# One root for layer 1's feed forward, and layer 2's twofold normalization moved into that feed forward

## The chip, the core and the metric

The kernel runs on one core of a Trainium2 chip. Its time is the device time of one execution in microseconds (us). The engines work side by side, each through its own list of instructions in order: TensorE (PE; its weight loads are shown as PEld), VectorE (DVE), ScalarE (ACT), GpSimd (POOL), and SyncE (SP), which issues the DMAs here. Semaphores tie the lists together.

## The reference

Four layers, each an attention-like part and a feed forward, every part added to `x` (4 batches, 1024 tokens, 128 features) after a layer normalization of `x`. What matters here is the end of layer 1 and the start of layer 2:

```
x = x + silu((LN(x) @ W_Q) @ W1 + b1) @ W2 + b2        # layer 1's outputs, with the trained W1, b1, W2, b2
g = softmax(LN(x) @ gate_w + gate_b)                    # 8 experts
g = where(g >= 0.1, g, 0); g = g / sum(g)
x = x + sum_e g[e] * (LN(x) @ expert_w[e] + expert_b[e]) # layer 1's feed forward
x = x + attention(LN(LN(x)) * gamma + beta)             # layer 2: normalized twice
```

W1, b1, W2 and b2 come out of a training loop over the sequence that runs just before (layer 1's "rounds").

## The kernel before

`x` stays on chip as 32 tiles of 128 tokens by 128 features; eight tiles are a batch. Beside it lies `xnT`, the normalized tokens turned so that features lie on partitions, which the matmuls read. All matrices are float32.

**A normalization** of one batch has two halves. `ln_moments` gets the sums (`ln_sums`: eight statistics instructions, L134, and five small operations, L137 to L141, on DVE), then the root: one ACT instruction (L114) and a reciprocal on DVE (L115), and `nm`, the shift (L125). With `twice` (layer 2) the second normalization is folded into the factor: six small operations on DVE (L117 to L122), a root on ACT (L123), and `nm`. `ln_scale` then scales eight tiles, four on ACT (L154) and four on POOL (L152), turns them on PE (L158, eight transposes into two PSUM tiles), and ACT copies the two results into `xnT` (L164, or L162 with gamma and beta). `self.ahead` keeps the sums that were made early.

**Layer 1's outputs** are the last part of `l1_attn`, in pools of their own (`l1o`, `l1q`). A preamble multiplies W_Q by W1 (L686 to L692) and spreads b2 (L694 to L700). Then eight blocks of 512 tokens: a product `hp` (L703), Silu on ACT (L705), b2 added on POOL (L169), four products `op` (L709), and the addition to `x` on DVE (`add_four`, L173).

**Layer 1's feed forward**, `l1_ffn`, opens its pools after that: two PSUM banks for transposes, one each for gates (`gp`), turned gates (`ap`) and biases (`bp`), three for experts (`ep`). For each batch it computes the gates (`weights`: sixteen-pass product L1014, then a softmax and threshold of small DVE operations L1019 to L1059, with Exp on ACT, L1024), adds the weighted biases (`biases`: L1065, L1067, L1070, L173), and for each of the eight tiles multiplies by all eight experts in two halves (L1081). Of the eight results, five are accumulated into `x` by DVE (L1090), three are weighted by ACT into `sc` (L1088) and added by POOL (L1092). The normalization of batch b + 1 stands ahead of batch b's tiles in the program.

**Layer 2's attention** begins with `layernorm(twice=...)`, again with its own pools (`ln`, `ln_ps`), and then projects batch 0 (L1205).

The order on each engine inside these parts is made by a planner: it takes the program's order as priority, and issues an instruction earlier where, by its own costs, an engine is free and the inputs and buffers are there. A pool opened later reuses the memory of a closed one, so its first writes wait for the last readers there. The attention itself is in an order written out by hand. ACT holds one table of functions at a time: Silu, Sqrt and Exp each have one; Copy and Identity run under any. A change of table is an instruction of its own (ACT_TABLE_LOAD), put before the function that needs it.

## Time and profile before

| | |
|---|---|
| median of 3 runs | 2631.39 us (2629.13 to 2631.81) |
| profiled execution | 2639.67 us |
| its span, first to last instruction | 2638.0 us |
| mean granted PE clock | 0.927 |
| first and last `op` product of layer 1's outputs (L709) | 827.8 and 841.4 us |
| first scaling of layer 1's feed forward (L154) | 846.84 us |
| first and last expert product (L1081) | 853.6 and 944.9 us |
| layer 2's first projection (L1205) | 957.24 us |

A group's row in the profile names line, engine, operation, output and inputs, how often, and the mean time of one. A row of a timeline begins with start and duration in us; several instructions of one kind in a row are merged (x8), and the brackets at the end say how long the engine had been idle before and what ended that. Lines are those of the kernel before; L158 and the like are helpers that several layers call.

ACT loads a table nine times between 818 and 924 us: at 818.24 (copy), 823.88 (Silu), 844.62 (root), 852.86 (Exp), 857.12 (root), 858.74 (Exp), 867.31 (root), 892.12 (Exp) and 923.23 (root), 1.28 us each.

### The profile page before, as it was taken

How to read it: one execution, taken by the hardware profiler on the slowest of the kernel's cores; microseconds unless marked ns; L12 is line 12 of the kernel's file. 1: busy time of each engine (PE TensorE's matmuls, PEld its weight loads, DVE VectorE, ACT ScalarE, POOL GpSimd, SP SyncE). 2: the span in 40 equal slices, each digit the busy share in tenths (PEclk: the TensorE clock that was granted, in tenths of full speed). 3: DMA queues.
4: the chain of work that ended last, by engine and by line, in shares of the span. 5: the costliest groups of instructions: out<-in, count | busy, mean ns of one | idle time of the engine just before them, and what ended most of it. 6: DMA issues, size and time to landing. Idle time of an engine off the chain costs nothing.

```text
span 2638.0 us, 51055 instructions
## 1 busy us (share of the span) xinstructions
PE 2384.1 (90%) x19913; PEld 1216.0 (46%) x19913; DVE 1793.4 (68%) x3670; ACT 1497.1 (57%) x3333; POOL 291.6 (11%) x525
## 2 busy tenths in 40 slices
PE   5688768899997979999999779999999999999878
PEld 4455435599996434333333443333333333333256
DVE  5889878466675767767775358767777777777343
ACT  4466458555554443666666635666666666656722
POOL 6012021000002440000000340000000000000011
PEclk8699879899998889999999879999999999999968
DMA  1333230000000000100010000000000000000000
GB/s 45 74 76 75 68 82 1 1 1 2 1 1 2 1 8 10 22 14 14 14 19 6 5 5 10 8 10 9 8 9 11 10 8 8 11 8 8 5 17 18
DMA packets 116719, 46.66 MB, mean 18 GB/s; under 512 B 88473, under 2 KB 111097, under 8 KB 116474
## 3 DMA queue, kind: packets, MB, share of 16 engines
q1 hardware_dynamic: 116474, 43.35, 8.3%
q8 instruction: 159, 2.61, 0.4%
q14 instruction: 86, 0.70, 0.1%
HBM read 17.04 MB, written 12.98 MB: 11 GB/s over the span
## 4 chain that ended last, share of the span: by engine, by line
PE 55%; DVE 4%; ACT 2%; POOL 1%; issue 1%; SPq 0%; DMA 0%; POOLq 0%; DVEq 0%; ACTq 0%
PE pb L1320 30%; PE po L1357 16%; PE pa L1265 2%; DVE bm L1277 1%; ACT es L1325 1%; PE pp L1205 1%; PE pe L1320 1%; DVE bm L1304 1%; PE pv L1186 1%; PE tp L158 1%; PE rp L1762 1%; PE gp L1014 1%; DVE bm L1308 0%; PE pr L1617 0%; PE kp L1530 0%
## 5 line engine op out<-in xcount | busy, mean ns | idle before, releaser
L1325 ACT ACTIVATE es<-pb 128x512 f32<-128x512 f32 x1462 | 795.7, 595 | 496.1 <-PE pb L1320 339.3
L1320 PE MATMUL pb<-q,k 32*128 32x512 f32 x2924 | 905.8, 640 | 3.2 <-DVE bm L1308 1.7
L1265 PE MATMUL pa<-k,q 32*128 32x512 f32 x2944 | 844.4, 648 | 10.2 <-DMA q<-q 10.2
L1277 DVE TENSOR_REDUCE bm<-pa 128x2 f32<-128x1024 f32 x496 | 604.6, 1224 | 260.5 <-PE pb L1320 168.0
L1357 PE MATMUL po<-es,v 128*32 128x256 f32 (+1 forms) x5760 | 474.8, 405 | 0.0
L1320 PEld LDWEIGHTS pb<-q,k 32*128 32x128 f32 x2924 | 295.3, 183 | 325.7 <-ACT es L1325 170.4
L1357 PEld LDWEIGHTS po<-es,v 128*32 128x32 f32 x5760 | 117.2, 108 | 528.7 <-issue 489.3
L1273 DVE TENSOR_REDUCE bm<-pa 128x16 f32<-128x1024 f32 x240 | 293.0, 1221 | 97.3 <-PE pb L1320 60.7
L1265 PEld LDWEIGHTS pa<-k,q 32*128 32x128 f32 x2944 | 233.5, 186 | 36.8 <-issue 18.5
L152 POOL TENSOR_SCALAR xn<-x,rs,nm 128x128 f32<-128x128 f32 x112 | 49.6, 459 | 1187.9 <-DVE nm L125 1013.7
L366 DVE TENSOR_TENSOR pr<-T,L 128x31 f32<-128x31 f32 (+15 forms) x248 | 91.7, 370 | 27.9 <-DMA L<-ld 20.6
L369 DVE TENSOR_TENSOR T<-T,pr 128x31 f32<-128x31 f32 (+15 forms) x248 | 93.1, 376 | 8.5
L158 PE MATMUL tp<-ident,xn 128*128 128x128 f32 x224 | 46.3, 357 | 42.5 <-ACT xn L154 38.0
L1364 DVE COPY oT<-po 128x512 f32<-128x512 f32 x48 | 32.7, 682 | 64.7 <-PE po L1357 64.7
L821 ACT ACTIVATE w<-tr,half 128x128 f32<-128x128 f32 x128 | 47.1, 368 | 48.3 <-PE tr L819 45.6
L796 ACT ACTIVATE a<-hp,wb 128x128 f32<-128x128 f32 x128 | 47.1, 368 | 41.6 <-PE hp L792 40.1
L1081 PE MATMUL ep<-L_ffn_expert_w,xnT 128*128 128x512 f32 x128 | 66.7, 653 | 3.3 <-DVE x L1090 3.0
L324 PE MATMUL wide<-bt,kt 32*128 32x128 f32 x512 | 30.4, 365 | 43.0 <-DVE mt L413 30.9
L486 PE MATMUL sp<-ux,kn 128*128 128x256 f32 x128 | 46.2, 494 | 17.8 <-ACT ux L475 17.7
L158 PEld LDWEIGHTS tp<-ident,xn 128*128 128x128 f32 x224 | 33.8, 178 | 60.4 <-ACT xn L154 46.9
L804 DVE TENSOR_TENSOR dlt<-gr,mask 128x128 f32<-128x128 f32 x96 | 28.0, 291 | 48.4 <-PE gr L802 48.1
L853 ACT COPY dr<-tr 128x128 f32<-128x128 f32 x128 | 34.1, 266 | 43.2 <-PE tr L851 41.1
(469 smaller groups left out, 3695.4 us busy)
## 6 DMA issues: line engine op xcount, KB each, us to landing
ld<-kk SPq DMA_DIRECT2D x128, 32.0 KB
L<-ld SPq DMA_DIRECT2D x8, 512.0 KB
td<-T SPq DMA_DIRECT2D x8, 512.0 KB
tb<-td SPq DMA_DIRECT2D x128, 32.0 KB
md<-nt SPq DMA_DIRECT2D x192, 2.0 KB
q<-md SPq DMA_DIRECT2D x192, 2.0 KB
x<-in_L_attn_x_dram SPq DMA_DIRECT2D x4, 512.0 KB
od<-o SPq DMA_DIRECT2D x32, 64.0 KB
```

The lines of the kernel that those rows point to most:

```text
L152: nc.gpsimd.tensor_scalar(xn[:, i, :], src[:, i, :], sl, bl, ALU.mult, ALU.add)
L158: nc.tensor.transpose(tp[:, i, :], xn[:, 4 * n + i, :], self.ident)
L366: nc.vector.tensor_mul(pv, T[:, 0 : j + 1, j : j + 1].to_broadcast(sh), L[:, j : j + 1, j + 1 :].to_broadcast(sh))
L369: nc.vector.tensor_sub(T[:, 0 : j + 1, j + 1 :], T[:, 0 : j + 1, j + 1 :], pv)
L796: nc.scalar.activation(self.a, self.hp, AF.Silu, bias=B1)
L1081: nc.tensor.matmul(ep.rearrange("p a b -> p (a b)"), lhsT=self.tok(t), rhs=ew[:, 4 * h : 4 * h + 4, :].rearrange("p a b -> p (a b)"), star ...
L1265: nc.tensor.matmul(pa[:, j % 2, :], lhsT=st["q"][r, i * P : (i + 1) * P], rhs=st["k"][r, n * 512 : (n + 1) * 512], start=True, stop=True,)
L1273: nc.vector.tensor_reduce(out[:, :, 1:9], pa.rearrange("p j (c s) -> p j c s", c=8), axis=AX.X, op=ALU.max)
L1277: nc.vector.tensor_reduce(out[:, :, n : n + 1], pa, axis=AX.X, op=ALU.max)
L1320: nc.tensor.matmul(pb, lhsT=st["k"][r, kc * P : (kc + 1) * P], rhs=st["q"][r, n * 512 : (n + 1) * 512], start=True, stop=True,)
L1325: nc.scalar.activation(es[turn][:, j, :], pb, AF.Exp, scale=scale)
L1357: nc.tensor.matmul(po[r, cols], lhsT=vring[b % 2][:, kc, 4 * g + j, :], rhs=es[:, j, cols], start=kc == 0, stop=True, skip_group_check=True,)
```

## The change

Layer 1's outputs move from `l1_attn` into a function `l1_out`, which gets the pools of the feed forward: `hp` uses the three `ep` buffers, `op` alternates between the buffers of `ap` and `bp`, and the preamble uses `gp`, `ap` and `bp`, with all its copies on DVE. `l1_ffn` calls it for two blocks (one batch) at a time, and after each batch takes that batch's sums. A new `ln_roots` makes the factors of several batches at once: one root, one reciprocal, one `nm` over all their columns. The feed forward's four normalizations use it with all four batches.

Layer 2's twofold normalization leaves `l2_attn`. The sums of batches 0 and 1 are taken in the feed forward during batches 1 and 2. After batch 2's tiles, `ln_roots` runs for batches 0 to 2 (with the sums of batch 2), and these three are scaled and turned ahead of batch 3's biases and tiles in the program. Batch 3 follows after its own tiles. These use the feed forward's pools: two PSUM banks for transposes in place of four.

```diff
+    def ln_roots(self, pool, bs, twice=None):
+        nc = self.nc
+        for b in bs:
+            if b not in self.ahead:
+                self.ln_sums(pool, b)
+        for b in bs:
+            del self.ahead[b]
+        rs, nm = (pool.tile([P, len(bs), TPB], F32, tag=f"{t}{len(bs)}", name=t) for t in ("rs", "nm"))
+        own = slice(bs[0], bs[-1] + 1)
+        q = self.sums[:, 1, own, :]
+        if twice is None:
+            nc.scalar.activation(rs, q, AF.Sqrt, bias=self.eps, scale=1.0 / D)
+            nc.vector.reciprocal(rs, rs)
+        else:
+            nc.vector.tensor_scalar(rs, q, 1.0 / D, EPS, ALU.mult, ALU.add)
+            nc.vector.reciprocal(rs, rs)
+            nc.vector.tensor_mul(q, q, rs)
+            nc.vector.tensor_scalar(q, q, 1.0 / D, EPS, ALU.mult, ALU.add)
+            nc.vector.reciprocal(q, q)
+            nc.vector.tensor_mul(rs, rs, q)
+            nc.scalar.activation(rs, rs, AF.Sqrt)
+        nc.vector.scalar_tensor_tensor(nm, self.sums[:, 0, own, :], -0.5, rs, ALU.mult, ALU.mult)
+        return [(rs[:, i, :], nm[:, i, :]) for i in range(len(bs))]
...
-        with tc.tile_pool(name="l1o", bufs=2) as two, tc.tile_pool(name="l1q", bufs=2, space=PSUM) as ps:
...
+    def l1_out(self, one, two, ps):
...
+        wqT = turned("gp", wq, [P, D])
+        b2r = turned("bp", B2, [1, D])
+        wp = ps.tile([P, D], F32, tag="ap", name="wp", bufs=1)
+        nc.tensor.matmul(wp, lhsT=wqT, rhs=W1, start=True, stop=True)
...
+        bp = ps.tile([P, D], F32, tag="gp", name="bp", bufs=1)
...
+        def batch(b):
+            for n in (2 * b, 2 * b + 1):
+                hp = ps.tile([P, 512], F32, tag="ep", name="hp", bufs=3)
                 nc.tensor.matmul(hp, lhsT=qw, rhs=self.tok(4 * n, 512), start=True, stop=True)
-                a = two.tile([P, 512], F32, tag="a", name="a")
+                a = two.tile([P, 512], F32, tag="a", name="a", bufs=2)
                 nc.scalar.activation(a, hp, AF.Silu, bias=B1)
                 self.add_bias(4 * n, b2)
-                op = ps.tile([P, 4, D], F32, tag="op", name="op")
+                op = ps.tile([P, 4, D], F32, tag=("ap", "bp")[n % 2], name="op", bufs=1)
                 for i in range(4):
                     nc.tensor.matmul(op[:, i, :], lhsT=a[:, i * P : (i + 1) * P], rhs=W2, start=True, stop=True)
                 self.add_four(4 * n, op)
...
-            self.ln_batch(ln, lps, 0)
+            out = self.l1_out(one, two, ps)
+            for b in range(NB):
+                out(b)
+                self.ln_sums(ln, b)
+            by = self.ln_roots(one, range(NB))
+            self.ln_scale(ln, lps, 0, by[0])
             g = weights(0)
             for b in range(NB):
                 if b + 1 < NB:
-                    self.ln_batch(ln, lps, b + 1)
+                    self.ln_scale(ln, lps, b + 1, by[b + 1])
                 biases(b, g)
+                if 0 < b < NB - 1:
+                    self.ln_sums(ln, b - 1)
                 for i in range(TPB):
                     tile_of(b * TPB + i, g[:, i, :])
                     if i == TPB // 2 and b + 1 < NB:
                         ahead = weights(b + 1)
                 g = ahead
+                if b >= NB - 2:
+                    done = range(NB - 1) if b == NB - 2 else (b,)
+                    twice = self.a2["gamma"], self.a2["beta"]
+                    by = self.ln_roots(one, done, twice)
+                    for i in done:
+                        self.ln_scale(ln, lps, i, by[i - done[0]], twice)
...
     def l2_attn(self):
         nc, a = self.nc, self.a2
         H, HD = 8, 16
-        self.layernorm(twice=(a["gamma"], a["beta"]))
```

## The prediction

> **What bounds the kernel now.** I read the page first, for the shares and for the clock row; then the table of stretches around the change; then the timelines of single engines there. The chain of waits is of no help for this place: followed back from the end it stops at 981.73 us, in layer 2's attention, so everything before that has to be read from timelines.
>
> ```profile
> PE 2384.1 (90%) x19913; PEld 1216.0 (46%) x19913; DVE 1793.4 (68%) x3670; ACT 1497.1 (57%) x3333; POOL 291.6 (11%) x525
> PEclk8699879899998889999999879999999999999968
> ```
>
> The program lives off TensorE (PE). The change touches only some 140 of its 2638 us, from the end of layer 1's rounds (817) to layer 2's first projection (957). That stretch, cut by what happens in it (columns: stretch, its length, then busy time and instructions of PE, weight loads, DVE, ACT, POOL, then the granted clock):
>
> ```profile
> 817.00:847.00 30.00, 19.29 (x86) 12.27 (x86) 11.01 (x44) 10.61 (x16) 10.80 (x9) 0.81 0.01 3
> 847.00:877.00 30.00, 27.82 (x83) 17.06 (x84) 15.14 (x71) 17.59 (x38) 9.62 (x22) 0.57 0.00 1
> 877.00:946.00 69.00, 64.27 (x162) 24.85 (x160) 58.44 (x234) 34.10 (x109) 42.27 (x94) 1.00 0.00 1
> 946.00:958.00 12.00, 6.62 (x33) 4.83 (x34) 5.56 (x28) 9.28 (x18) 6.94 (x17) 0.73 0.01 2
> ```
>
> From 847 to 946 PE is busy 92.1 of 99 us, DVE close behind after 877. PE is the bound of the experts' stage; before and after it lie two waits for a normalization (841.4 to 847.4, 944.9 to 957.2). From 847 to 877 PE works at 0.57 of its clock. Finer rows:
>
> ```profile
> 844.00:847.00 3.00, 0.00 (x0) 0.00 (x0) 3.00 (x24) 2.02 (x4) 0.00 (x0) 0.78 0.00 0
> 859.00:862.00 3.00, 2.38 (x18) 1.93 (x16) 0.59 (x5) 1.02 (x1) 0.00 (x0) 0.94 0.00 0
> 862.00:865.00 3.00, 1.87 (x3) 0.63 (x3) 2.59 (x12) 2.02 (x8) 1.74 (x4) 0.63 0.00 0
> 874.00:877.00 3.00, 3.00 (x5) 1.14 (x5) 1.75 (x5) 1.61 (x6) 1.36 (x3) 0.60 0.00 0
> 877.00:880.00 3.00, 3.00 (x16) 1.94 (x15) 1.57 (x5) 1.45 (x6) 1.36 (x3) 1.00 0.00 0
> ```
>
> The clock falls at about 845.3, comes back at about 859.3, falls again at about 862.8 and is back for good at about 875.8.
>
> **Part A, the first wait.** Before, the statistics of layer 1's feed forward begin only when the last output has been added:
>
> ```profile
> 841.50 0.69 DVE L173 TENSOR_TENSOR x<-op,x 128x512 f32<-128x512 f32 x1 [0.20 <-PE op L709]
> 842.11 1.83 DVE L134 BATCH_NORM_STATS2 st<-x 128x6 f32<-128x128 f32 x9
> 844.62 1.28 ACT L114 ACT_TABLE_LOAD   x1 [4.47 <-DVE sums L140]
> 846.84 2.03 ACT L154 ACTIVATE xn<-x,nm,rs 128x128 f32<-128x128 f32 x5
> ```
>
> Sums of batch 0 are there at 844.52; then a load of ACT's table, a root (0.30), a reciprocal, nm, and the first scaling at 846.84. Afterwards each batch's sums follow its own two output blocks. One batch is eight statistics at 0.207 (the pitch of the 1.83 for nine) plus five small operations in 0.66 (843.86 to 844.52), 2.3 in all. DVE idles 2.17 before every second addition (830.9, 834.7, 838.4), so batches 0 to 2 fit almost exactly; without that cover they would cost 3 x 2.3 = 6.9. The last batch's 2.3 stays behind the last addition: 842.1 + 2.3 = 844.4. One root over 32 columns is 0.3 and a hand-over 0.1; its table load can run right behind the last Silu (840.15), since nothing else is due on ACT; reciprocal and nm 0.4: scaling from 845.2, **-1.7**. If the load stays behind the wait, as it did at 844.62, it is 846.5, -0.3; if four statistics slip in ahead of the last addition, 844.4, -2.5.
>
> A rule weighed: the Trainium skill ("ScalarE: Activation LUTs", What ACT_TABLE_LOAD costs) counts a change of table at 1.28 us plus a drain of about 1.38. The row shows 1.28, and the root began at 845.92, 0.02 behind the load's end: no drain. By the page part A would be -3.1, and the five loads that go (nine between 818 and 924 become four: Silu, root, Exp, root) would free 13.3 us of ACT; by the row -1.7 and 6.4. I take the row. The five that go are priced at nothing: the one at 818 lies in idle time, the three at 857 to 869 beside matmuls at low clock, which fill PE to 861.4 and again from 863.6, the one at 892 in ACT's slack (34 of 69 us busy). Uncovered they would be 1.28 each.
>
> **The preamble** (two transposes, two products, four copies now all on DVE) keeps its length: 0.27 on ACT, 0.28 on DVE for a copy. Output blocks get three buffers in place of two for their first product; PE sets that pace (3.9 per pair of blocks) before and after, 0. The eight loads of the experts' biases and the 0.94 memset stand ahead of the outputs now, but ran at 821 to 825 already, beside the preamble: 0.
>
> **Part B, the clock.** From 847.4 PE does the same work 1.7 earlier. Its gap shrinks from 6.0 to about 4.2; the clock fell 3.9 after the last output product, so it probably falls again. The skill ("TensorE: Matmul & The Clock Gate", Part 1) lets it fall after an idle window of about 3.4 us and return after 3.4 us of sustained matmuls. PE was busy nearly without pause from 847.4, and the clock came back at 859.3, 12 us on; again 12 from 863.6 to 875.8. What precedes both returns is 4.7 to 5.8 us of mostly 512-column expert products; transposes and eight-column gate products seem not to count. By the page both cold stretches together cost 2 x 1.7 and little can be won; by the rows 13 us of the second stretch run at half speed, 6.4 lost. Whether it vanishes hangs on one thing: at 855.98 DVE had batch 0's gates half done and then stood 5.39 behind batch 1's gate sum (L1019), which waited for PE. That sequence is the planner's, which sees all four scalings available at once. I take **0**; ends -6.4 (no second fall) and +3 (more short work gathered in the cold part).
>
> **Part C, DVE while experts run.** Small operations: 28 of the twofold chain become 14, at 0.12 pitch -1.7 on an engine that is 85% busy; PE waited for it 3.0 in all, so -0.7. Against it: the sums of batches 0 to 2 now come ahead of the next batch's accumulations, and a statistic of a batch's last tile waits for POOL's additions; DVE waited so once for 0.5 here, and 2.5 at layer 2's attention. Behind it stand the accumulations that free PE's banks. Three such waits, +0.7. Together **0**, ends -1.7 and +3.
>
> **Part D, the twofold scaling among the last batch's tiles.** Before, three quarters of it ends the stage:
>
> ```profile
> 946.67 1.97 PE L158 MATMUL tp<-ident,xn 128*128 128x128 f32 x16 [1.77 <-DVE x L1090]
> 947.37 2.79 ACT L162 ACTIVATE xnT<-tp,L_attn_beta,L_attn_gamma 128x512 f32<-128x512 f32 x4 [1.48 <-PE tp L158]
> 950.70 1.64 ACT L154 ACTIVATE xn<-x,nm,rs 128x128 f32<-128x128 f32 x4
> 952.34 1.63 ACT L162 ACTIVATE xnT<-tp,L_attn_beta,L_attn_gamma 128x512 f32<-128x512 f32 x2
> 953.87 1.64 ACT L154 ACTIVATE xn<-x,nm,rs 128x128 f32<-128x128 f32 x4
> 957.24 3.78 PE L1205 MATMUL pp<-xnT,L_attn_Wk 128*128 128x512 f32 x4 [0.87 <-ACT xnT L162]
> ```
>
> Afterwards batches 0 to 2 are done under batch 3's tiles. Moved there: 24 transposes (1.97 for 16) = 2.95 on PE; 12 scalings at 0.41 and six evictions at 0.78 = 9.6 on ACT; 12 scalings at 0.43 = 5.2 on POOL. Batch 3 already holds 22.3 of PE time (922.6 to 944.9, idle 1.6), 7 of ACT and 12.2 of POOL. PE is the bound, so 2.95 is added. The scalings stand ahead of batch 3's tiles in program order, so ACT's nine to ten us can hold back sc (0.87 a tile), and sc holds a bank of PE's three. Best: PE's idle time takes half of the transposes, +1.4. Worst: ACT runs the block whole, +12.5. PE can run about 1.5 tiles (3.3) ahead. I take **+3.5**, near the low end, because ACT has 36.2 us of waiting for PE in this stage to give.
>
> **Part E, the last wait.** Batch 2's scaling and evictions (950.70 to 953.87) leave the path, 3.2; POOL's four scalings at 942 no longer delay the last additions (nine in a row to 948.22), 0.2: **-3.4**, ends -2.5 and -4.5. Statistics, chain and root of batch 3 stay. Attention's start stays: its first product needs the banks of the last transposes either way.
>
> **Sum:** -1.7 + 0 + 0 + 3.5 - 3.4 = -1.6 us. The profiled execution took 2639.67 (span 2638.0, 1.67 around it): 2638.1, span 2636.4. The median runs stand 8.3 below the profiled one; the same -1.6 gives **2629.8**. A measurement of this kernel tells about 0.2% (5.3 us) from no change.
>
> **Rivals.** (1) *No second fall of the clock*: batch 0's gates finish before PE runs dry, -1.6 - 6.4 = -8.0, 2623.4. For it: nothing of layer 1's sums is left in DVE's way after 845. Against: gates and transposes of later batches may be pulled forward into the same place. (2) *Slower: ACT's block starves PE in batch 3.* If the block runs unbroken, PE stops 9.6 - 3.3 = 6.3 beside the 2.95; a pause of over 3.3 in expert products drops the clock (859.7 to 862.8), and the next 4.7 run at half speed, +2.4. Part D is then 11.7, the sum +6.6, 2638.0. It decides from a pause of 3.3 on; below that the sum is under +3. For it: ACT put four scalings in one run at 925.55 (1.65). Against: evictions must wait for transposes, and sc fills those holes. (3) *It doesn't do what it says*: the transposes stay behind the last expert product, as at 946.67, and only part A comes: 2629.7, or a little slower through part C.
>
> **How the numbers follow.** Forecast 0.45 (faster 0.05, same 0.38, slower 0.02), rival 1 0.24 (0.21 faster, 0.03 same), rival 2 0.20 (0.17 slower, 0.03 same), rival 3 0.11 (0.07 same, 0.04 slower): faster 0.26, same 0.51, slower 0.23. The forecast's own range is 2626 to 2634; with rivals 1 and 2, 2622 to 2638.5.
>
> **What would show it.** Right: statistics between 830 and 841, one root of 32 columns, first scaling near 845.2; four table loads; transposes of layer 2's batches 0 to 2 between expert products; only batch 3's scaling between the last expert product and the first projection, about 9 us apart instead of 12.3. Wrong: a pause over 3.3 in expert products in batch 3, or a clock row of 1.00 from 860 on.

## The result, and the profile after

The changed kernel is slower: 2642.2 us (median of 9 runs) against 2634.27 us for the kernel before, run beside it (9 runs). The ratio is 1.0032, with a 95% interval of 1.0020 to 1.0045, which is +5 to +12 us. The forecast was 2629.8, with a range up to 2638.5. The profiled execution took 2645.73 us (span 2644.0), the one before 2639.67 (2638.0).

The page's first rows and its clock row, after the change:

```profile
PE 2379.7 (90%) x19913; PEld 1213.6 (46%) x19913; DVE 1794.4 (68%) x3652; ACT 1489.5 (56%) x3321; POOL 292.2 (11%) x525
PEclk8699779899998988999999878999999999999968
```

These totals hide the change: a stage of 140 us out of 2640 doesn't show in them. The table of stretches does. It is cut at the same events as the four stretches shown before (the whole stage begins 1.9 us later in this profile):

```profile
818.90:848.90 30.00, 19.65 (x88) 11.99 (x88) 16.92 (x67) 8.75 (x13) 11.19 (x10) 0.81 0.01 3
848.90:878.90 30.00, 27.27 (x110) 17.14 (x110) 13.92 (x55) 15.93 (x42) 11.68 (x28) 0.84 0.00 1
878.90:956.30 77.40, 64.41 (x160) 24.39 (x158) 54.08 (x215) 34.50 (x105) 41.38 (x93) 0.98 0.00 1
956.30:968.00 11.70, 4.03 (x11) 1.93 (x11) 5.35 (x18) 4.30 (x10) 6.69 (x13) 0.69 0.00 1
```

Look at three columns. In the first row DVE has 16.9 us of work where it had 11.0: the statistics lie beside the outputs. In the second row the granted clock is 0.84 in place of 0.57: the second fall of the clock is gone in this profile. In the third row PE does the same 64.4 us of work (64.3 before), but the stretch is 77.4 us long in place of 69. PE's idle time there went from 4.7 to 13.0 us, so **PE no longer bounds the experts' stage**.

To add this up, all positions below count from the preamble's first transpose (821.97 before, 823.85 after). What lies ahead of it differed by up to 5.6 us between profiles, and what follows layer 2's first projection by up to 7.2 us; neither is touched by the change. "Tile n" is the start of the third weighting of that tile on ACT (`sc`).

| kernel | first scaling | tile 0 | tile 0 to 25 | tile 25 to 31 | tile 31 to first projection | first projection | low clock after 40 us | time, ratio to before (95%) |
|---|---|---|---|---|---|---|---|---|
| before | 24.87 | 41.95 | 69.28 | 12.33 | 11.72 | 135.27 | 13.7 | 1 |
| after | 24.58 | 40.19 | 69.75 | 23.12 | 9.03 | 142.08 | 0 | 1.0032 (1.0020 to 1.0045) |
| e1 outputs alone | 24.57 | 40.44 | 65.66 | 12.07 | 20.02 | 138.20 | 6.8 | 1.0002 (0.9992 to 1.0012) |
| e2 twofold alone | 24.97 | 42.10 | 79.51 | 24.17 | 8.67 | 154.45 | 13.7 | 1.0048 (1.0033 to 1.0063) |
| e3 sums held | 24.56 | 40.42 | 70.31 | 23.12 | 9.03 | 142.87 | 6.8 | 1.0022 (1.0010 to 1.0035) |
| e4 scalings spread | 24.58 | 40.31 | 72.38 | 21.37 | 8.47 | 142.53 | 10.2 | 1.0019 (1.0011 to 1.0027) |
| e5 no block | 24.57 | 40.36 | 71.94 | 16.88 | 9.03 | 138.20 | 6.8 | 0.9996 (0.9981 to 1.0011) |
| e6 held and spread | 24.57 | 41.71 | 75.02 | 18.45 | 9.20 | 144.38 | 13.7 | 1.0013 (0.9998 to 1.0028) |
| e7 outputs, room | 24.56 | 40.35 | 68.58 | 12.91 | 12.64 | 134.48 | 6.8 | 0.9991 (0.9980 to 1.0002) |
| e8 outputs, late sums | 24.57 | 40.36 | 65.04 | 12.25 | 17.05 | 134.70 | 6.8 | 0.9995 (0.9981 to 1.0009) |
| e9 last sums held | 24.58 | 40.11 | 69.79 | 20.56 | 8.47 | 138.93 | 0 | 1.0010 (0.9996 to 1.0023) |
| e10 layer 2 last | 24.58 | 40.33 | 66.55 | 12.31 | 13.78 | 132.97 | 10.2 | 0.9989 (0.9978 to 1.0000) |
| e11 layer 2 last, copies on ACT | 24.55 | 40.19 | 66.53 | 12.32 | 13.78 | 132.82 | 10.2 | 0.9991 (0.9978 to 1.0004) |
| e12 roots in last batch | 24.59 | 40.33 | 66.35 | 15.78 | 12.71 | 135.17 | 10.2 | 0.9996 (0.9984 to 1.0008) |

The stage is 142.08 - 135.27 = 6.8 us longer, which is the loss: **tile 25 to 31 alone lost 10.8**, the last wait won 2.7, the rest 1.3. The column of low clock is the time at half of PE's clock, in the trace's clock records, in the stretch that begins at about 41 us. It is partly chance: after, e4, e5 and e9 have the same instructions in the same order up to tile 24 and differ only in this from tile 0 to 25 (69.7 and 69.8 with none; 71.9 with 6.8; 72.4 with 10.2). So a microsecond of low clock costs about 0.3 there, an estimate; e8 and e10, alike up to tile 8 (24.90 and 26.22 with 6.8 and 10.2), give 0.4. A difference of under some 3 us between two profiles is read with that in mind.

**Where tile 25 to 31 went.** The timeline of the changed kernel, PE, then ACT, POOL and DVE, around layer 2's scaling of batches 0 to 2:

```profile
942.32 1.02 PE L1116 MATMUL ep<-L_ffn_expert_w,xnT 128*128 128x512 f32 x2
943.18 1.13 PE L183 MATMUL tp<-ident,xn 128*128 128x128 f32 x6
944.92 0.82 PE L183 MATMUL tp<-ident,xn 128*128 128x128 f32 x4 [0.61 <-ACT xn L179]
947.27 4.38 PE L1116 MATMUL ep<-L_ffn_expert_w,xnT 128*128 128x512 f32 x6 [1.53 <-DVE x L1125]
...
937.80 1.65 ACT L179 ACTIVATE xn<-x,nm,rs 128x128 f32<-128x128 f32 x4 [0.94 <-DVE nm L150]
945.14 1.44 ACT L187 ACTIVATE xnT<-tp,L_attn_beta,L_attn_gamma 128x512 f32<-128x512 f32 x2
946.47 1.90 ACT L1123 ACTIVATE sc<-ep,g 128x128 f32<-128x128 f32 x7
...
937.95 5.16 POOL L177 TENSOR_SCALAR xn<-x,rs,nm 128x128 f32<-128x128 f32 x12 [0.85 <-DVE nm L150]
...
940.54 1.51 DVE L1125 SCALAR_TENSOR_TENSOR x<-ep,g,x 128x128 f32<-128x128 f32 x4 [1.35 <-PE ep L1116]
946.87 0.35 DVE L1125 SCALAR_TENSOR_TENSOR x<-ep,g,x 128x128 f32<-128x128 f32 x1 [4.81 <-ACT sc L1123]
```

ACT's twelve scalings and six evictions run as one block from 937.80 to 946.6. No weighting comes between them, so DVE waits 4.81 for one, the three banks stay full, and PE makes no expert product from 943.34 to 947.27 (a product is two instructions in the trace, a tile four). The granted clock then falls (columns as in the table of stretches):

```profile
943.00:946.00 3.00, 2.13 (x11) 0.95 (x9) 0.00 (x0) 3.00 (x8) 0.11 (x1) 1.00 0.02 5
946.00:949.00 3.00, 1.73 (x2) 0.83 (x3) 0.85 (x3) 2.37 (x8) 1.54 (x4) 0.66 0.00 0
```

From 943 to 946 ACT is busy all of the time and DVE none of it.

**The second loss is spread over all tiles.** DVE's statistics in groups, first before (870 to 960 us), then after (the same window):

```profile
L134 DVE BATCH_NORM_STATS2 st<-x 128x6 f32<-128x128 f32 x32 | 8.8, 279 | 0.5 <-POOL x L1092 0.5
```

```profile
L159 DVE BATCH_NORM_STATS2 st<-x 128x6 f32<-128x128 f32 x32 | 9.3, 292 | 20.9 <-POOL x L1127 20.7
```

The same 32 instructions waited 0.5 us for POOL before, and 20.7 after. A single tile shows how:

```profile
906.80 1.51 POOL L1127 TENSOR_TENSOR x<-x,sc 128x128 f32<-128x128 f32 x3 [1.14 <-DVE x L1125]
...
908.35 0.29 DVE L159 BATCH_NORM_STATS2 st<-x 128x6 f32<-128x128 f32 x1 [0.98 <-POOL x L1127]
908.56 0.72 DVE L1125 SCALAR_TENSOR_TENSOR x<-ep,g,x 128x128 f32<-128x128 f32 x2
```

POOL may begin a tile's three additions only when DVE has done its five, and they take 1.51. The statistic of that tile stands on DVE a few accumulations later, so DVE stands still until POOL is through. In the kernel before, layer 2's first statistic came at 76.2 us, 26 us after its tile was complete (50.6), and the others of batches 0 to 2 came 11 to 26 us behind theirs; now the first comes at 47.4, and each follows its tile.

**The front.** The changed kernel's timeline, DVE and then ACT, to be held against the first fence of part A:

```profile
834.86 0.39 DVE L162 TENSOR_TENSOR d<-st 128x8 f32<-128x8 f32 x1
835.17 1.30 DVE L163 TENSOR_TENSOR sums<-st 128x8 f32<-128x8 f32 x1
844.75 0.67 DVE L198 TENSOR_TENSOR x<-op,x 128x512 f32<-128x512 f32 x1
847.26 0.17 DVE L165 TENSOR_TENSOR sums<-sums,d 128x8 f32<-128x8 f32 x1
...
828.27 1.28 ACT L738 ACT_TABLE_LOAD   x1 [12.39 <-PE hp L736]
842.67 1.28 ACT L140 ACT_TABLE_LOAD   x1
847.46 0.32 ACT L140 ACTIVATE rs<-sums,eps 128x32 f32<-128x32 f32 x1 [3.51 <-DVE sums L165]
848.43 2.04 ACT L179 ACTIVATE xn<-x,nm,rs 128x128 f32<-128x128 f32 x5 [0.65 <-DVE nm L150]
```

The root's table load does run right behind the last Silu (842.67) and is hidden. But the last addition starts at 20.90 us after the first transpose, where it was at 19.53. Two things happened there, and part A below says which decides. Silu's own table load now stands behind the first `hp` (12.39 of waiting, then 1.28) because ACT has no copy in the preamble any more; the last output product ends 0.6 later. And one `sums` instruction of batch 0 took 1.30 where its fellows take 0.17: it ended at 836.47, and POOL's run of eight bias additions (1.23 each) at 836.45:

```profile
826.60 9.85 POOL L194 TENSOR_TENSOR x<-x,b 128x512 f32<-128x512 f32 x8 [2.37 <-DVE b L731]
```

**The end.** After the change, from the last expert product on, PE, DVE and ACT:

```profile
955.19 1.10 PE L1116 MATMUL ep<-L_ffn_expert_w,xnT 128*128 128x512 f32 x2 [0.74 <-DVE x L1125]
963.10 1.97 PE L183 MATMUL tp<-ident,xn 128*128 128x128 f32 x8 [6.81 <-ACT xn L179]
965.93 2.08 PE L1254 MATMUL pp<-xnT,L_attn_Wk 128*128 128x512 f32 x2 [0.87 <-ACT xnT L187]
...
959.84 0.29 DVE L159 BATCH_NORM_STATS2 st<-x 128x6 f32<-128x128 f32 x1 [1.63 <-POOL x L1127]
962.55 1.65 ACT L179 ACTIVATE xn<-x,nm,rs 128x128 f32<-128x128 f32 x4 [0.24 <-DVE nm L150]
```

Only batch 3's normalization is left: 9.65 us from the end of the last expert product to the first projection, in place of 12.33.

### The profile page after: what moved, and what is told of

Its sections match the earlier page's. It is cut to its first block, busy times and chain, and to the rows that moved or that the text cites. A ratio compares the mean times of both kernels' runs of the same rounds, so it can differ in the third digit from the quotient of the medians.

```text
span 2644.0 us, 51019 instructions
## 1 busy us (share of the span) xinstructions
PE 2379.7 (90%) x19913; PEld 1213.6 (46%) x19913; DVE 1794.4 (68%) x3652; ACT 1489.5 (56%) x3321; POOL 292.2 (11%) x525
## 4 chain that ended last, share of the span: by engine, by line
PE 55%; DVE 4%; ACT 2%; issue 1%; POOL 1%; SPq 0%; DMA 0%; POOLq 0%; DVEq 0%; ACTq 0%
PE pb L1369 30%; PE po L1406 16%; PE pa L1314 2%; ACT es L1374 1%; DVE bm L1326 1%; PE pp L1254 1%; PE pe L1369 1%; DVE bm L1353 1%; PE rp L1810 1%; PE pv L1235 1%; PE tp L183 1%; PE gp L1049 1%; DVE bm L1357 0%; PE pr L1665 0%; PE rp L1587 0%
## 5 line engine op out<-in xcount | busy, mean ns | idle before, releaser
L159 DVE BATCH_NORM_STATS2 st<-x 128x6 f32<-128x128 f32 x224 | 51.9, 281 | 30.4 <-POOL x L1127 20.7
```

The lines of the kernel that those rows point to most:

```text
L159: nc.vector.bn_stats(st[:, i, :], self.x[:, b * TPB + i, :])
```

## The experiments

All diffs are against the changed kernel unless another is named. `tc.issue_after(x)` makes what is issued inside it stand behind `x` on its engine; `dve`, `act` and `pool` are the last accumulation, weighting and addition of a tile, handed back by `tile_of`.

**e1 and e2: each half of the change alone.** e1 keeps the outputs in the feed forward, and layer 2 normalizes in its attention as before; e2 is the kernel before plus the twofold part.

```diff
 # e1
-                if 0 < b < NB - 1:
-                    self.ln_sums(ln, b - 1)
...
-                if b >= NB - 2:
-                    ...
 # in l2_attn
+        self.layernorm(twice=(a["gamma"], a["beta"]))
```

> Layer 1's part alone; layer 2's twofold normalization is back at the head of layer 2, as before. Measure: the stretch from the preamble's first transpose to layer 2's first projection, 135.3 us in the kernel before, 142.1 in the changed one, and the time. Theory A (the loss is all in the twofold part): statistics ahead and a clock that does not fall a second time stay, so 127 to 130 us, time 5 to 8 us below before (ratio 0.997 to 0.998). Theory B (sharing pools and banks costs part of it): 135 or more, ratio 1.000 or above.

> The kernel before with the twofold normalization inside the feed forward, layer 1's outputs and the four roots as before. Theory A: the twofold part costs about 14 us by itself (142.1 minus the 128.5 expected of the other part), so a stretch of 147 to 150 us and a ratio of 1.004 to 1.006, with DVE waiting behind POOL in statistics and a pause of expert products in batch 3. Theory B: it costs 7 or less, 142 us or below.

The loss is the twofold part's; e7 below clears the other half. e2 costs 0.48% by itself: tile 0 to 25 grew by 10.2 us with the same low clock as before, tile 25 to 31 by 11.8. In its profile the stage is 19.2 us longer, more than expected, while its time is 12.7 longer (8.7 to 16.6), as expected. The rest of the program makes the difference: what follows the first projection took 1674.5 us in e2's profile and 1680.7 in the one before, with 148.2 and 162.7 us of low clock in it.

By its numbers e1 came out as theory B foresaw, but it holds two opposite things: it won 5.4 us up to the last expert product and lost 8.3 behind it, with 20.0 from tile 31 to the projection, where the kernel before has 11.7. Its timeline, DVE and ACT:

```profile
942.22 1.84 DVE L159 BATCH_NORM_STATS2 st<-x 128x6 f32<-128x128 f32 x9
...
948.12 1.65 ACT L179 ACTIVATE xn<-x,nm,rs 128x128 f32<-128x128 f32 x4 [0.32 <-DVE nm L125]
```

All 32 statistics of layer 2 now begin when the last accumulation is over (942.2), although three batches had been complete for long. No wait for data explains this. The feed forward's first pool had become smaller, since the roots' outputs lie in another one, and layer 2's pool of the same kind may now lie on memory that the experts use to the end. e7 tests that.

**e7: the same with room.** e1, with the roots' outputs in the pool that held them before.

```diff
 # against e1
-            by = self.ln_roots(one, range(NB))
+            by = self.ln_roots(ln, range(NB))
```

> Layer 1's part alone (the first experiment), with the roots' outputs in the pool of the normalization, so that layer 2's normalization pool covers the same memory as before and no tile of the experts. If the 20 us from the last sc to layer 2's projection came from memory that the experts held to the end, they fall to 11 to 13, and the statistics run among the experts' tiles again, preamble to projection 129 to 133. If not, they stay at 20.

One argument moved the statistics back into the experts' stage and took 7.4 us out of the tail (20.0 to 12.6), so the place of the buffers had been the cause; which memory was waited for, the trace doesn't show. The stage, 134.5, stayed above the 129 to 133 expected. It also brought back some of what they cost there: tile 0 to 25 is 2.9 longer than in e1. The time is 0.9991 (0.9980 to 1.0002): the outputs' half alone, placed so, costs nothing, and what it may win (up to 0.2%) can't be told from no change.

**e3: batches 0 and 1's statistics held.** They stand behind tile 1 of the next batch, when POOL is through with all of theirs.

```diff
-                if 0 < b < NB - 1:
-                    self.ln_sums(ln, b - 1)
                 for i in range(TPB):
-                    tile_of(b * TPB + i, g[:, i, :])
+                    dve, act, pool = tile_of(b * TPB + i, g[:, i, :])
+                    if i == 1 and 0 < b < NB - 1:
+                        with tc.issue_after(dve):
+                            self.ln_sums(ln, b - 1)
```

> The changed kernel; on DVE the sums of batches 0 and 1 are queued behind tile 1 of the next batch, so that the statistics don't follow a tile by one. Some 14 of 24 waits of DVE for POOL (20.7 us in all) go. Theory A1 (these waits cost the experts' stage time): 4 to 6 us shorter, a stretch of 136 to 138. Theory A2 (DVE has that time to give, only the block of scalings in batch 3 costs): within 1.5 us of 142.1.

The groups on DVE in e3, from 866 to 958 us:

```profile
L1125 DVE SCALAR_TENSOR_TENSOR x<-ep,g,x 128x128 f32<-128x128 f32 x158 | 48.9, 343 | 17.0 <-ACT sc L1123 14.0 <-PE ep L1116 1.6 <-DVE x L1125 0.2
L159 DVE BATCH_NORM_STATS2 st<-x 128x6 f32<-128x128 f32 x30 | 7.4, 283 | 7.4 <-POOL x L1127 7.3
```

The wait for POOL fell from 19.1 to 7.3 in this window, but the wait for ACT's weightings rose from 5.5 to 14.0. Held at this priority, the eight statistics of a batch come in one lump of 1.64 on DVE, and the experts stop behind it once a batch:

```profile
898.17 3.67 PE L1116 MATMUL ep<-L_ffn_expert_w,xnT 128*128 128x512 f32 x8 [2.43 <-DVE x L1125]
```

From tile 0 to 25 e3 took 70.3 in place of 69.7. Corrected for 6.8 us of low clock at 0.3 each, which only e3 had, that is about 1.5 better, and the stage stayed within 1.5 us of the changed kernel's, as theory A2 has it. So waits of 12 us were taken away for less than 2 us of gain. That DVE waits 20.7 us doesn't mean that 20.7 were lost.

**e4: the block spread.** Each of the three scalings stands behind the weightings and additions of tiles 1, 3 and 5 of batch 3.

```diff
...
+                    if b == NB - 1 and i in (1, 3, 5):
+                        with tc.issue_after(act), tc.issue_after(pool):
+                            self.ln_scale(ln, lps, i // 2, by[i // 2], twice)
...
-                    for i in done:
-                        self.ln_scale(ln, lps, i, by[i - done[0]], twice)
+                    if b == NB - 1:
+                        self.ln_scale(ln, lps, b, by[0], twice)
```

> The changed kernel; the scalings of batches 0, 1 and 2 are queued on ACT and POOL behind tiles 1, 3 and 5 of batch 3 and no longer run as one block. Theory A1: the pause between expert products (from 940.3 to 947.3 only two) goes, with the fall of the clock after it: 5 to 8 us shorter, a stretch of 134 to 137. Theory C (ACT has too much work in batch 3 whatever its order): less than 3 us shorter, 139 or more.

Tile 25 to 31 shrank by 1.75 only, as theory C foresaw. ACT's block is gone, but PE works its list in order, and the transposes wait for POOL's half of the scalings, with expert products behind them:

```profile
944.95 1.62 PE L183 MATMUL tp<-ident,xn 128*128 128x128 f32 x7 [0.90 <-POOL xn L177]
...
951.60 1.61 PE L183 MATMUL tp<-ident,xn 128*128 128x128 f32 x7 [1.42 <-POOL xn L177]
```

So the cost is not only that the work comes in one piece. Four engines pass each tile around in a circle here (PE, ACT and DVE, POOL, DVE's statistic), and here work put on POOL stops PE.

**e5: no block.** This kernel leaves out the twofold scaling, the transposes and the evictions of batches 0 to 2 (their `xnT` stays the one from layer 1), and keeps everything else of the change.

```diff
-                    for i in done:
-                        self.ln_scale(ln, lps, i, by[i - done[0]], twice)
+                    if b == NB - 1:
+                        self.ln_scale(ln, lps, b, by[0], twice)
```

> The changed kernel without the twofold scaling, turning and eviction of batches 0 to 2 (left out: layer 2's normalized input of these three batches; the tokens stay as layer 1 normalized them). Their root and the statistics stay. Measure: from the third sc of tile 25 to the third sc of tile 31, 12.3 us in the kernel before and 23.1 in the changed one. Theory A (the block of scalings alone makes batch 3 long): 13 to 16 us, and 7 to 10 us less time. Theory D (DVE's statistics that wait for POOL in batch 3 make half of it): 17 to 20.

Tile 25 to 31 is 16.88, nearest to theory D: the block is worth 6.2 of the 10.8. The other 4.6 stay without any block, and e5's timeline shows what most of them are (PE, then DVE):

```profile
943.04 1.96 PE L1116 MATMUL ep<-L_ffn_expert_w,xnT 128*128 128x512 f32 x4 [1.53 <-DVE x L1125]
945.73 1.96 PE L1116 MATMUL ep<-L_ffn_expert_w,xnT 128*128 128x512 f32 x4 [0.73 <-DVE x L1125]
...
945.04 0.29 DVE L159 BATCH_NORM_STATS2 st<-x 128x6 f32<-128x128 f32 x1 [0.98 <-POOL x L1127]
```

A tile takes 2.69 (943.04 to 945.73) instead of 2.06 in the kernel before (12.33 for six): DVE waits 0.98 for POOL at the tile's statistic, and PE waits 0.73 for DVE. Six tiles make 3.8 of the 4.6 so.

**e9: only batch 3's statistics held**, behind the last tile, with the block whole.

```diff
                     twice = self.a2["gamma"], self.a2["beta"]
+                    if b == NB - 1:
+                        with tc.issue_after(dve):
+                            self.ln_sums(ln, b)
                     by = self.ln_roots(one, done, twice)
```

> The changed kernel, only batch 3's statistics for layer 2 stand behind the last tile's accumulations on DVE instead of one tile behind POOL; the block of scalings stays whole. If the two costs in batch 3 are separate (block 6.2 us, statistics behind POOL 4.6), tile 25 to tile 31 takes 23.1 - 4.6 = 18.5 us, the statistics then lengthen the way to the first projection by 0.5 to 1.7, and the time is about 3 us below the changed kernel, 1.001 to 1.002 of the kernel before. If the block alone sets the pace and the statistics only fill the holes that it makes, tile 25 to 31 stays at 22 to 23 us and the time at 1.003.

20.56, between the two expectations: 2.6 won where 4.6 was to come. The two costs overlap; while the block stops the experts, no statistic is late. Held so, batch 3's statistics cost the tail nothing (8.47 to the projection in place of 9.03); the last of them waits 0.27 for POOL instead of 1.63.

**e6: statistics held and scalings spread.** Sums of batches 0 to 2 behind tile 1 of the next batch, of batch 3 behind the last tile; one root for batches 0 and 1, another for 2; scalings behind tiles 0, 2 and 5 of batch 3.

```diff
...
+                    if i == 1 and b > 0:
+                        with tc.issue_after(dve):
+                            self.ln_sums(ln, b - 1)
+                    if b == NB - 1 and i == TPB - 1:
+                        with tc.issue_after(dve):
+                            self.ln_sums(ln, b)
+                    if b == NB - 1 and i in (0, 2, 5):
+                        with tc.issue_after(act), tc.issue_after(pool):
+                            m = i // 2
+                            if m == 2:
+                                by = by + self.ln_roots(one, (2,), twice)
+                            self.ln_scale(ln, lps, m, by[m], twice)
...
```

> The changed kernel with the scalings of batches 0, 1 and 2 spread behind tiles 0, 2 and 5 of batch 3, and every batch's sums held on DVE: those of 0 to 2 behind tile 1 of the next batch, those of batch 3 behind its last tile; batch 2's factors are made by themselves. If spreading failed to help because statistics that wait for POOL stood between DVE, POOL and the transposes, the stretch from tile 25 to tile 31 falls from 21.4 to 15 to 18 us, and preamble to projection from 142 to 134 to 137. If it failed because the transposes of a spread scaling wait in PE's order for POOL, it stays at 20 or more.

Tile 25 to 31 is 18.45, just above the 15 to 18 of the first expectation, better than each cure alone and still 6.1 above before. The stage, 144.4 where 134 to 137 was foreseen, is a miss. Tile 0 to 25 is the longest but one of the table: the lumps of eight statistics stopped PE for 2.4 in batches 1 and 2, and in this profile the clock fell after both (two tiles' products at 901.17 and at 922.55 took 5.37 each, where 3.67 is the rule). The time, 1.0013, can't be told from before.

**e8: the outputs' half, with late statistics.** e7, with the sums of batches 0 to 2 still taken in the feed forward, but behind the next batch's tiles in the program, so that they only fill holes, and not ahead of tile 1.

```diff
 # against e7
...
+                if b > 0:
+                    with tc.issue_after(late):  # tile 1's last accumulation
+                        self.ln_sums(ln, b - 1)
...
```

> As the experiment before it in this call, and layer 2's sums of batches 0 to 2 are traced after the next batch's tiles and queued on DVE behind that batch's tile 1, so that they fill gaps and never follow a tile at once. Expected from the parts: to tile 0 as in the changed kernel (40.3), 66 to 68 to tile 25, 12.3 to tile 31, 11.7 to the projection: 130 to 132.5 us against 135.3, ratio 0.998 to 0.9995. If sums among the tiles cost what they cost in the changed kernel wherever they stand: 134 or more, ratio 1.000.

This gives the shortest experts' stage of all: tile 0 to 25 in 65.04, with statistics that wait 0.0 for POOL. Against the changed kernel that is 4.7 less as measured, and 6.7 less with e8's 6.8 us of low clock taken off at 0.3 each: **the early statistics cost about 7 us** from tile 0 to 25, by this estimate. (Of the 24 statistics that the changed kernel has there, e8 leaves 8 for later; its tile 25 to 31 is no longer for it, 12.25.) But the tail is 17.0 and the stage 134.7, which by the number alone is the second expectation, since layer 2's chains begin only at the end, and two of them stand behind a scaling, because two buffers hold four batches' factors:

```profile
944.59 0.17 DVE L117 TENSOR_SCALAR rs<-sums 128x8 f32<-128x8 f32 x1 [1.79 <-POOL xn L177]
947.30 0.17 DVE L117 TENSOR_SCALAR rs<-sums 128x8 f32<-128x8 f32 x1 [1.37 <-ACT xn L179]
```

**e10 and e11: all of layer 2 at the lowest priority.** Late sums as in e8, and roots (batches 0 and 1, then 2, then 3), scalings and transposes behind batch 3's tiles in the program, in the feed forward's pools. e11 also gives the preamble's copies of W_Q and of its product with W1 back to ACT.

```diff
...
+            with tc.issue_after(dve):  # the last tile's
+                self.ln_sums(ln, NB - 1)
+            twice = self.a2["gamma"], self.a2["beta"]
+            for bs in ((0, 1), (2,), (3,)):
+                by = self.ln_roots(one, bs, twice)
+                for i in bs:
+                    self.ln_scale(ln, lps, i, by[i - bs[0]], twice)
...
```

> The changed kernel, with layer 2's sums of batches 0 to 2 behind the next batch's tile 1, those of batch 3 behind the last tile, and the roots (batches 0 and 1 together, 2, 3) and all scalings and transposes behind batch 3's tiles in the program, in the feed forward's pools. If what cost the changed kernel is only the place of statistics and scalings, the last expert product comes 117 to 118 us after the preamble's first transpose (122.9 before), batches 0 and 1 are scaled by the time the experts end, and the first projection follows in 12 to 13: about 130 in place of 135.3 before, 0.998 of its time. If low priority again makes the chain of batch 3 start late, as when the sums alone were late, the tail is 17 or more and the time the same as before.

> The same, with the copies of turned W_Q and of its product with W1 on ACT, as in the kernel before, in place of DVE. If Silu's table load was exposed because ACT had nothing to do before the first hp, it now runs beside the preamble, outputs end 0.6 us earlier and everything behind moves by 0.6 (first scaling 24.0 us after the first transpose instead of 24.6). If DVE's additions and statistics (3.5 us a batch) set the pace of the outputs, the first scaling stays at 24.4 to 24.6.

e10's experts' stage is nearly as foreseen (12.31 for the last six tiles; the last expert product ends at 118.6), and the projection comes at 132.97, 2.3 ahead of before and 9.1 ahead of the changed kernel. From the last expert product to the projection it takes 14.4, where 12 to 13 was foreseen. Its timeline shows why (POOL, then DVE):

```profile
937.21 3.48 POOL L177 TENSOR_SCALAR xn<-x,rs,nm 128x128 f32<-128x128 f32 x8
940.66 3.00 POOL L1127 TENSOR_TENSOR x<-x,sc 128x128 f32<-128x128 f32 x6
...
942.21 0.29 DVE L159 BATCH_NORM_STATS2 st<-x 128x6 f32<-128x128 f32 x1 [1.38 <-POOL x L1127]
943.69 0.29 DVE L159 BATCH_NORM_STATS2 st<-x 128x6 f32<-128x128 f32 x1 [1.19 <-POOL x L1127]
```

Eight scalings stand ahead of the last six additions on POOL, and batch 3's last two statistics wait 2.6 in all for them. The measured ratio is 0.9989 (0.9978 to 1.0000): the best of the study, and too small to be called a gain.

e11's last output product ended 0.5 earlier (19.64 against 20.18), so Silu's load had been exposed; but the first scaling did not move (24.55 against 24.58). In both runs it comes 11.98 after the end of POOL's bias additions, which sets the end of the first sums.

**e12: roots inside batch 3.** Late sums; the common root of batches 0 to 2 behind tile 3 of batch 3, batch 0's scaling behind tile 4, those of batches 1 and 2 behind tile 7.

```diff
...
+                    if b == NB - 1 and i == 3:
+                        with tc.issue_after(late):
+                            self.ln_sums(ln, b - 1)
+                        with tc.issue_after(dve):
+                            by2 = self.ln_roots(one, (0, 1, 2), twice)
+                    if b == NB - 1 and i == 4:
+                        with tc.issue_after(act), tc.issue_after(pool):
+                            self.ln_scale(ln, lps, 0, by2[0], twice)
...
```

> The changed kernel, with layer 2's sums of batches 0 to 2 behind tile 1 of the next batch, the common root of batches 0 to 2 behind tile 3 of batch 3, batch 0's scaling behind tile 4's last weighting (ACT) and last addition (POOL), and batches 1 and 2's behind tile 7's; batch 3's sums behind tile 7. In the run before, POOL's eight scalings ahead of the last tile's additions held the last statistics back 2.6, and batch 2's shift stood behind batch 3's chain on DVE. If that is what kept its tail at 14.4, tile 25 to 31 stays at 12.2 to 13, the last expert product at 118 to 119, the tail falls to 10 to 11 and the first projection comes at 129 to 130 (135.3 before): 0.998 of the time before. If batch 0's scaling alone already holds back the last tiles on POOL and PE, tile 25 to 31 is 14 or more, the projection comes at 132 or later and the ratio is 0.999.

The second expectation came: 15.78 for the last six tiles, projection at 135.17, ratio 0.9996. Both holes on PE are DVE's (the first one ends with the root's chain), and the chain for batch 3 waits for its root on ACT, behind batch 1 and 2's scalings (DVE's row last):

```profile
938.22 2.81 PE L1116 MATMUL ep<-L_ffn_expert_w,xnT 128*128 128x512 f32 x6 [1.47 <-DVE sums L145]
942.19 1.10 PE L1116 MATMUL ep<-L_ffn_expert_w,xnT 128*128 128x512 f32 x2 [1.16 <-DVE x L1125]
...
955.16 0.17 DVE L150 SCALAR_TENSOR_TENSOR nm<-sums,rs 128x8 f32<-128x8 f32 x1 [3.37 <-ACT rs L149]
```

Even one batch's scaling and a chain of eight small operations cost 3.5 us inside the last tiles, and the tail won only 1.1 for it against e10. No version here beats both kernels by more than the measurement can tell.

## Why the prediction was wrong

Two steps failed: part D, which took ACT's idle time for room (+3.5 predicted, +10.8 measured), and part C, which let the early statistics wait for POOL three times (+0.7, balanced to 0), where they waited 20.7 us in all and, by the estimate below, lengthened the stage by 4.5 to 5.8. The stage moved by -0.3 - 5.5 + 4.5 + 10.8 - 2.7 = +6.8 us; the prediction had -1.7 + 0 + 0 + 3.5 - 3.4 = -1.6.

**Part A (-1.7 predicted, -0.3 measured: mis-sized).** The mechanism came: statistics beside the outputs, one root, its load hidden. It sat at the weak end that the prediction named, for another reason than the load of the root. In all twelve profiles with the outputs moved, the first scaling comes 11.97 to 11.99 after the end of POOL's bias additions, while the last output product ends anywhere from 19.64 to 20.29. Batch 0's first sums end with POOL's run, and from there to batch 3's last sum DVE has no pause: a batch there is 3.54 of work (836.75 to 840.29), with PE at 3.75 (834.34 to 838.09), so "fit almost exactly" left nothing to catch up with. The Trainium skill ("SBUF — State Buffer", SBUF: two separate sides) says that a DVE operation with two inputs in SBUF and a GpSimd operation that reads SBUF exclude each other for a whole instruction. This case agrees, in the same twelve profiles: the first two such operations of batch 0 (L162, L163) end 0.02 to 0.06 after the seventh and the eighth of POOL's bias additions, and L163 takes 1.28 to 1.31 in place of 0.17. Silu's load, exposed by moving the preamble's copies off ACT, which "keeps its length" had priced at nothing, made the outputs 0.6 later, but e11 shows that it does not decide: without it, outputs 0.5 earlier, first scaling where it was. The prediction moved DVE's sums past POOL's queue without looking at what POOL was doing there.

**Part B (0 predicted, ends -6.4 and +3; about -5.5 in this profile).** The outcome of rival 1, which the prediction gave 0.24, came in this profile: the second fall of the clock is missing. Its mechanism did not come. Batch 0's gates again stood half done behind batch 1's gate sum on DVE, and PE again ran dry before them, though for less time, since transposes of a later batch now stand in that place (the first row is of the kernel before, the others of the changed one):

```profile
862.78 0.42 PE L1065 MATMUL ap<-ident,g 128*64 128x128 f32 x1 [1.40 <-DVE g L1059]
863.03 0.30 PE L1100 MATMUL ap<-ident,g 128*64 128x128 f32 x1 [0.48 <-DVE g L1094]
861.66 0.23 DVE L1054 TENSOR_TENSOR g<-gp,L_ffn_gate_b 128x64 f32<-128x64 f32 x1 [4.04 <-PE gp L1049]
```

All twelve profiles with this front have the 0.48, and in ten of them the clock fell all the same, for 6.8 to 13.7. So the missing fall was luck, and other runs of the changed kernel will mostly have won less here than this profile. The -5.5 is 1.5 up to tile 0, where the first low stretch lasts 10.2 in place of 13.7 (in e6 it lasts 13.7 again, with tile 0 at 41.7), and about 4 behind it (13.7 us at 0.3, an estimate from the profiles above). The Trainium skill ("TensorE: Matmul & The Clock Gate", Part 1) has the clock return after about 3.4 us of sustained matmuls; here the rows were the right guide, since PE had no pause from 847.39 on and the clock came back 12.0 later. The rows were read a little short, though: by the clock's records the two stretches before are 845.7 to 859.4 and 862.8 to 876.4, 13.7 each, not 845.3 and 875.8 at their outer ends, and half of the second is 6.8, not 6.4.

**Part C (0 predicted, +4.5 measured: the step that failed first).** The failing sentence is "Three such waits, +0.7". The prediction let only a batch's last tile wait for POOL, and took 0.5 of waiting, from a kernel in which most statistics came 11 to 26 us behind their tiles, as if that were the rule for statistics that follow at once. Measured: 20.7 us of waits, and about 7 us of length against e8. Against the kernel before the estimate is 69.75 - (69.28 - 13.7 x 0.3) = 4.5, less than 7, since there DVE had layer 2's chains and sums to do late in this stretch, too. At 0.4 for a microsecond of low clock part C is 5.8 and part B -6.8; their sum, -1.0, is measured. What to ask of a step that is moved nearer to its input is how far behind the input it will then stand.

**Part D (+3.5 predicted, +10.8 measured: the largest error).** The worst end was +12.5, and rival 2 had 11.7. Its mechanism is what the traces show: the block ran whole (8.8 us against 9.6), expert products paused for 3.9 (the point of decision was 3.3), the clock fell and the next three products took 4.38, where three take 2.8 (938.22 in e12). The argument that ACT has 36.2 us of waiting to give failed: that time lies in 25 pieces of 1.4 us on average between ACT's turns on the tiles, and e4 shows that work cut to fit them still costs. But rival 2 is not all of it. e5 without any block keeps 4.6 of the 10.8, most of which are batch 3's own statistics behind POOL, part C's error once more. By e9 they are 2.6 when the block is there. Block and statistics overlap, so their shares are ranges: 6.2 to 8.2 and 2.6 to 4.6. That rival 2's 11.7 lies so near to 10.8 is partly luck.

**Part E (-3.4 predicted, -2.7 measured): right**, within its ends. The 9.65 stand against the "about 9" that was foreseen. Most of the missing 0.7 has a row: the last statistic waits 1.63 for POOL (0.45 before), and e9, where it waits 0.27, has 0.6 less to the projection.

**The sum.** Of the 12.4 us between 2629.8 and 2642.2, 2.9 belong to the base: the kernel before has 2634.27 in nine runs, where the forecast started from 2631.39 in three. Rival 2 was priced at 2638.0 and would have been nearest. Its chance of 0.20 was too low because slack was counted as a total over the stage. Part C's upper end (+3) was too low as well. Rival 3 did not come: the 24 transposes stand between expert products, the four table loads are as foretold.

What stays open: why the twofold part costs 10.2 us from tile 0 to 25 in e2 and only some 4 to 7 beside the moved outputs, and what decides how long the second low stretch of the clock lasts.

## What to carry to other kernels

Idle time of an engine in a loop where several engines hand each tile around was not room for other work here: an engine that waited 1.4 us at a time took in no block, and in e4 and e12 even small pieces stopped the others. When an operation is moved nearer to its producer, count its distance to the producer after the move; statistics right behind POOL cost about 7 us in 25 tiles (an estimate), and late and at low priority they waited 0.0. Moving a small buffer from one pool to another can shift when a later stage may begin, by 7.4 us here, without a wait in the trace that names it.

## What the runs showed of the hardware

- In all 14 traces every record of PE's granted clock but the last one lasts a whole multiple of 3.413 us; the low stretches of this stage have 3.4 to 34.1. With the same instructions in the same order to tile 24, the low stretch at 41 us lasted 0, 0, 6.8 and 10.2. A microsecond of it costs about 0.3 to 0.4 us there, estimated from these and from e8 and e10.
- One of DVE's sums with two inputs in SBUF took 1.28 to 1.31 us in place of 0.17 when POOL was adding 128 x 512 tiles, and ended with POOL's instruction, in twelve profiles. The time is inside DVE's instruction and not in its idle time. The additions from PSUM (L198, 0.67 to 0.69) beside the same run were not held.
- A table load stood behind its function's wait once (828.27, after 12.39 of waiting) and ahead of it another time (842.67, 4.8 ahead of the root). What decides it, the runs don't show.
